# A graph network layer on one Trainium2 core: one more product by quarters in three weight matrices, a shared PSUM bank, and half of a count moved

## The chip, the cores and the metric

The kernel runs on one core of one Trainium2 chip. A core has TensorE (PE, the matrix unit), VectorE (DVE), ScalarE (ACT), GpSimd (POOL) and SyncE (SP); each works through its own instructions in order, and they wait for each other by semaphores. TensorE writes its products to PSUM, eight banks of 512 float32 columns on 128 partitions, and VectorE and ScalarE take them from there. Transfers between memory and the core's SBUF are DMAs, issued from the queues of SP, ACT and POOL. The metric is device time in microseconds (us) of one execution; lower is better. The time before is 1338.05 us, the median of three runs (1337.94 to 1341.44).

## What is computed

Rows of x are normalised and rectified to h. For each of eight edge types r, the rows of h at the sources of the edges of that type are averaged at each destination and multiplied by `weight[r]`; with `h @ root` and the bias that gives u. Then come a gate and a residual.

```python
h = jnp.maximum(_layernorm(x), 0.0)              # 1250 x 1024
out = h @ root + bias
for r in range(8):                               # 20000 edges, 8 types
    mask = (edge_type == r).astype(h.dtype)
    sums = segment_sum(h[src] * mask[:, None], dst, num_segments=1250)
    cnt = segment_sum(mask, dst, num_segments=1250)
    out = out + (sums / jnp.maximum(cnt, 1.0)[:, None]) @ weight[r]
u = out
z = jnp.concatenate([u, h], axis=1) @ w_gate + b_gate
result = x + jnp.tanh(u) * z + h * (1.0 - z)
```

## The kernel before

**Products first, gathers after.** The kernel multiplies h by each weight matrix first, stores the products y, and then gathers rows of y for the edges. Matrices 0 to 7 are `weight[0..7]`, matrix 8 is `root`, 9 and 10 are the lower and upper half of `w_gate`. The edges fall into two groups: group 0 has types 0 to 4, group 1 types 5 to 7 (`R0 = (0, 5, 8)`), so group 0 can be gathered after matrix 4, while TensorE is at matrices 5 to 7.

**One step.** The 1250 rows are ten blocks of 128 (the last one shorter). Step (m, i) multiplies blocks i and i + 5 by matrix m, for i = 0 to 4. It uses Strassen's scheme in Winograd's form: the two blocks and the halves of the inner dimension make a 2 x 2 left operand (A11, A12, A21, A22 and the sums S1 to S4, kept in `h_op`), the matrix is cut in four quarters of 512 x 512 (B11 to B22 and the sums T1 to T4), and seven products replace eight. A product is four matmuls 512 columns wide, all at L406. `product` writes them in a fixed order: A11·B11, S1·T1, S2·T2, S3·T3 and so on to A22·T4. ScalarE evicts some results to the row tiles (L457 the first, L469 S1, L489 S2, L430 S3, L529 A22), VectorE adds the others (L423, L431, L448). A row tile's half c21 holds S3's result for L431 and then gets A22's from L529.

**A second level.** In matrices 1 to 9 steps 0 and 1, and 2 and 3, make pairs. Some of their products are done for both steps of a pair at once, by quarters, by the same scheme again: seven products of two matmuls 256 columns wide (L219) in place of two products of four. `Second` does A12·B21 that way and `First` A11·B11, in all paired steps; `Third` does S4·B22, only where `thirds(s)` says so, which is s > EARLY = 3. Elsewhere S4·B22 is a plain product (`p3`, L423). The quarter products need sums of quarters from VectorE: L273 to L282 for `Third` and `First`, L207 to L215 for `Second`. `Third.first` (called from the `fill` of step 1 or 3) makes three quarter products in two banks: P1 into bank `ps_q`, copied out by ScalarE (L297); S1·T1 into a bank of the pool `ps`; S2·T2 onto P1 in `ps_q`, copied out by ScalarE (L300). `Third.last` adds three more, and `fifth_to`, `first_to` and `last_to` add the results to the rows on VectorE (L308 to L317). `First.early` and `First.late` seed a bank by ScalarE (L345, L355), and TensorE accumulates onto the seed.

**Calls.** After each product (and some fillers) `product` runs `between(j)`, j = 0 to 6; the step's `beside(j)` then issues the sums and weight loads that stand at that j and calls whatever other work runs beside the products. The order of the products, and with it the place of a call, depends on what the step has: where `first` is given, `head` is set and the fill has no "first", half of S1 comes first, then `First.late` and call 0; where the fill has a "first", S1 and call 0 come before `First.late`.

**The index.** From matrix 0 on, beside the products, `slots` gives each edge its place in a table of slots, 40 chunks of 512 edges. Each takes two phases, one a call. The first has `one_hots` (ScalarE, L1055, L1057; VectorE, L1060), loads of keys (SP) and `as_bf16` (ScalarE, L1102). The second has `look` and `count` (TensorE, bf16 matmuls into `ps_q`, L1124, L1069), `pick` and `add_counts` (VectorE, which read `ps_q`, L1132, L1077), `residue`, `place` (VectorE, L1140, L1145, and every fourth time the scatter of 16 columns of edges by GpSimd, L1163) and `to_los` (ScalarE, L1116, L1117). From matrix 1 on nothing of it is done at calls (0,0), (1,5) and (4,4). Then `order` sorts the destinations: `places` is twenty VectorE rows over 1280 columns (L1205), ten for each group, one a call; after each group GpSimd writes and reads the positions (L788, L798) and gathers the slots of the nodes (L740, `idx`). The index ends in step (4,1).

**Counts, weights, gathers.** `counts(g)` counts the edges of each node by type from `idx` (VectorE, L777, L778), `as_reciprocals` inverts the counts, `weights(g)` makes a weight for every slot. Counts of both groups run in matrix 4; then `counts_over` loads a register on every engine and skips a conditional (`tc.If`, L1533) that is for nodes with more edges than slots; then the weights run in matrices 4 and 5. From call (5,0,3) on GpSimd gathers rows of y (`add_slot`, L1339), into five buffers `got`, and VectorE adds them to u with their weights (L1344).

**Buffers.** PSUM has four banks `ps` and two `ps_b` in rotation, and `ps_n` and `ps_q`. In matrices 1 to 3 `ps_q` belongs to the index and `ps_n` is not used.

Of the kernel before, what the change touches and what calls it, by code (L numbers as in the profile page):

```python
# [19 lines left out]
def tile_rgcn_highway(  # L20
# [238 lines left out]
    class Third:  # L259
# [31 lines left out]
        def first(self, p):  # L291
            self.b = psum.tile([P, CG, P], F32, name="ps_q", bufs=1).rearrange(
                "p c k -> p (c k)")[:, :H]
            self.c = bank()[:, :H]
            self.p = p
            Second.add(self, self.b, self.a11, self.b11, True)
            nc.scalar.copy(self.p[:, :H], self.b)  # L297
            Second.add(self, self.c, self.s1, self.t1, True)
            Second.add(self, self.b, self.s2, self.t2)
            nc.scalar.copy(self.p[:, H:], self.b)  # L300

        def last(self, c):
            Second.add(self, self.b, self.s1, self.t1)
            Second.add(self, self.c0[:, H:], self.s2, self.b22)
            Second.add(self, c[:, :H], self.a22, self.t2)
# [5 lines left out]
        def fifth_to(self, to):  # L311
            nc.vector.tensor_add(to[:, H:], to[:, H:], self.c)

        def last_to(self, to, to1, c):
# [236 lines left out]
    def thirds(s):  # L551

        return s > EARLY

# [3 lines left out]

    waiting, waiting_third, waiting_first = {}, {}, {}
    at_call = [0, 0]  # L560

# [8 lines left out]
    def step(s, i, between=lambda j: None, second=None):  # L570
# [23 lines left out]
        def beside(j):  # L594
            at_call[:] = i, j
            new = fac[s + 1]
# [39 lines left out]
        def sums(j):  # L636


            e = waiting[0][0]
            for k in {2: (0, 1), 5: (2, 3)}.get(j, ()) if s > EARLY else (j,) if j < 4 else ():  # L640
                e.right(k)
            if j == (5 if s > EARLY else 4):
                e.next_left()
# [13 lines left out]
        if two:  # L657
# [98 lines left out]
    def slot_weights(g, at, w, t, drc):  # L756

        n = at.shape[2]
        for r in range(R0[g], R0[g + 1]):
# [50 lines left out]
    with ExitStack() as early:  # L810
# [161 lines left out]
        at_i = ix1.tile([P, NCH], I32, name="at_i")  # L972
        q_bank = psum.tile([P, CG, P], F32, name="ps_q", bufs=1).rearrange("p c k -> p (c k)")

# [60 lines left out]
        def slots(ix):  # L1035
# [6 lines left out]
            ng = -(-NCH // CG)  # L1042
            counted = q_bank[:, H:H + CG * NHI].rearrange("p (c b) -> p c b", b=NHI)
            looked = q_bank[:, H + CG * NHI:H + 3 * CG * NHI].rearrange(
                "p (c a b) -> p c a b", a=2, b=NHI)
# [136 lines left out]
        def order():  # L1182

            with tc.tile_pool(name="sort", bufs=1) as sp:
# [11 lines left out]
                nc.vector.memset(one, 1.0)  # L1196
                for _ in range(7):
                    yield
                pos = sp.tile([P, NHI], F32, name="pos")

                def places(g):
                    for d in range(ND):
# [4 lines left out]
                            op0=OP.is_gt, op1=OP.mult, accum_out=pos[:, c:c + 1])  # L1207
                        yield
                    nc.vector.tensor_copy(pos_i[:, g, :], pos[:, g * ND:(g + 1) * ND])
# [10 lines left out]
        def norms():  # L1220
# [59 lines left out]
            first_part.close()  # L1280

        def index():
            for _ in zip_longest(norms(), columns()):
# [23 lines left out]
    with ExitStack() as edges_part:  # L1307
# [18 lines left out]
        def counts(g):  # L1326
            t = got()
# [4 lines left out]
        def as_reciprocals():  # L1332
            nc.vector.tensor_scalar_max(rcp, rcp, 1.0)
            nc.vector.reciprocal(rcp, rcp)

# [111 lines left out]

        def beside(e, total, s, i, last):


            between = spread(e, total, 7 * ((last - s) * NP + NP - i))
            while s <= last:
                step(s, i, between)
                s, i = next(steps, (NM, 0))
            return s, i

        s, i = next(steps)
        while s <= EARLY:
            step(s, i)
            s, i = next(steps)  # L1460

        def beside_group():
# [3 lines left out]
            for _ in range(5):  # L1466
                yield
            for g in range(G):
                yield from counts(g)

        def weights_of_groups():

            as_reciprocals()
            yield
            for g in range(G):
                yield from weights(g)
                yield
            yield from passes_needed()

# [48 lines left out]

        def counts_over():

            over = nc.values_load(n_over[0:1, 0:1], min_val=0, max_val=E // MORE,
                                  skip_runtime_bounds_check_because="no more passes than edges")
            with tc.If(over > 0):  # L1533
                p = Passes()
                with tc.For_i(0, over, 1):
                    p.to_table()
                    for g in range(G):
                        slot_rows(g, more_rows, p.at)
                        for _ in slot_counts(g, p.at, p.t, p.cum, p.more):
                            pass  # L1540
                    nc.vector.tensor_add(rcp, rcp, p.more)
                    p.next()
# [6 lines left out]
        while s < R0[1]:  # L1549
            step(s, i, on)  # L1550
            s, i = next(steps)
            if (s, i) == (R0[1] - 1, NP - 1):
                for _ in ready:
                    pass
                counts_over()
                ready = weights_of_groups()

# [251 lines left out]
```

## Time and profile before

| | |
|---|---|
| median of three runs | 1338.05 us |
| the profiled execution's own time | 1337.41 us |
| its span | 1335.6 us |
| granted TensorE clock | 0.998 of full |

Windows of the profiled execution, from step (m, 0) to the next matrix (us; each engine's busy time in it):

| matrix | window | PE | DVE | ACT | POOL |
|---|---|---|---|---|---|
| 1 | 143.0 to 265.0 | 122.0 | 74.5 | 70.4 | 66.5 |
| 2 | 265.0 to 387.0 | 122.0 | 77.0 | 70.6 | 68.7 |
| 3 | 387.0 to 505.5 | 118.5 | 69.3 | 24.1 | 44.3 |
| 4 | 505.5 to 621.4 | 115.9 | 67.1 | 20.8 | 39.5 |
| 5 | 621.4 to 737.2 | 115.8 | 98.0 | 20.9 | 52.4 |

The profile has the execution of one core. "Busy" is the time in which an engine has an instruction running; L406 is line 406 of the kernel. In a timeline each line has the start, the busy time, engine, line, operation, output and inputs, shapes and how many; what stands in brackets is the idle time before it and what ended it. A float32 matmul has two records, so a product of four matmuls shows as x8. An instruction's busy time overlaps the next one's start by about 0.1 us.

### The profile page before, as it was taken

The page shows a single profiled execution, that of the slowest core. Times are in us where ns is not written, and L with a number is a line of the kernel's source. Part 1 is how long each engine was busy: PE and PEld are TensorE (multiplying, and loading weights), DVE is VectorE, ACT ScalarE, POOL GpSimd, SP SyncE. Part 2 cuts the span into 40 slices and gives each one's busy share as a digit, 9 for nine tenths or more (in the row PEclk, how much of TensorE's full clock was granted, in tenths as well). Part 3 has the DMA queues.
Part 4 walks back from the last instruction along what each step waited for, and adds up shares of the span by engine and source line. Part 5 has one row for each costly group of instructions (what it writes and reads, how often), then busy time and mean ns, then how long its engine had stood idle before and what let it go on. Part 6 is the DMA issues. An engine that isn't in the chain of part 4 may idle for free.

```text
span 1335.6 us, 13410 instructions
## 1 busy us (share of the span) xinstructions
PE 1323.3 (99%) x4168; PEld 722.1 (54%) x4168; DVE 956.9 (72%) x1823; ACT 372.7 (28%) x794; POOL 568.5 (43%) x509
## 2 busy tenths in 40 slices
PE   9999999999999999999999999999999999999997
PEld 5444555455455545655655565565556556544443
DVE  7753755674675467448987978897778889867875
ACT  3335556465641212111121121112121112221210
POOL 0000364554657036501454546346365555615631
PEclk9999999999999999999999999999999999999999
DMA  8745476866754241143738778878788957969961
GB/s 318 270 182 175 104 124 141 191 126 109 172 160 95 88 114 53 53 148 111 254 127 319 244 253 333 290 238 268 277 273 301 347 192 243 308 251 296 340 168 59
DMA packets 104319, 270.94 MB, mean 203 GB/s; under 512 B 20100, under 2 KB 22354, under 8 KB 104112
## 3 DMA queue, kind: packets, MB, share of 16 engines
q1 hardware_dynamic: 44048, 119.85, 29.3%
q0 software_dynamic: 44064, 118.20, 27.7%
q10 hardware_dynamic: 16128, 31.98, 7.7%
q8 instruction: 33, 0.54, 0.2%
q14 instruction: 46, 0.38, 0.1%
HBM read 212.63 MB, written 75.49 MB: 216 GB/s over the span
## 4 chain that ended last, share of the span: by engine, by line
PE 85%; issue 4%; DVE 2%; DMA 2%; POOL 1%; ACT 0%; POOLq 0%; DVEq 0%; ACTq 0%
PE ps_b L406 41%; PE ps L406 17%; PE ps L219 14%; PE ps_b L219 4%; PE ps_n L406 4%; PE ps_q L219 2%; PE ps_n L219 2%; PE ps_q L406 2%; DMA w<-in_L_gnn_b_gate_dram 1%; DMA h_op<-z_dram,node 1%; POOL out_dram L746 1%; DVE row L1733 0%; DVE row L1734 0%; PE ps_q L1069 0%; PE ps_q L1124 0%
## 5 line engine op out<-in xcount | busy, mean ns | idle before, releaser
L406 PE MATMUL ps_b<-w,h_op 128*128 128x512 f32 x1464 | 659.6, 595 | 1.0 <-ACT row L489 0.8
L406 PEld LDWEIGHTS ps_b<-w,h_op 128*128 128x128 f32 x1464 | 273.6, 190 | 308.4 <-issue 297.4
L1339 POOL DMA_INDIRECT got<-y,idx x193 | 245.8, 1274 | 290.3 <-DVE u L1344 184.1
L1344 DVE SCALAR_TENSOR_TENSOR u<-got,w_of,u 128x1024 f32<-128x1024 f32 (+1 forms) x193 | 246.9, 1282 | 31.8 <-DMA got<-y,idx 29.3
L406 PE MATMUL ps<-w,h_op 128*128 128x512 f32 (+1 forms) x592 | 264.8, 589 | 0.1
L1163 POOL DMA_INDIRECT table<-row_col,at_i x157 | 165.2, 1052 | 185.5 <-DVE at_i L1159 133.0
L406 PEld LDWEIGHTS ps<-w,h_op 128*128 128x128 f32 x592 | 111.0, 190 | 119.2 <-issue 115.0
L431 DVE TENSOR_TENSOR row<-row 128x512 f32<-128x512 f32 x44 | 30.3, 690 | 79.0 <-ACT row L430 79.0
L430 ACT COPY row<-ps_b 128x512 f32<-128x512 f32 x53 | 31.1, 586 | 194.1 <-PE ps_b L406 194.1
L406 PE MATMUL ps_n<-w,h_op 128*128 128x512 f32 x176 | 80.1, 592 | 0.0
L489 ACT COPY row<-ps_b 128x512 f32<-128x512 f32 x54 | 31.7, 586 | 163.6 <-PE ps_b L406 163.4
L219 PE MATMUL ps<-w,h_op 128*128 128x256 f32 x288 | 74.5, 381 | 0.0
L219 PE MATMUL ps<-w,w 128*128 128x256 f32 x288 | 71.1, 380 | 0.0
L529 ACT COPY row<-ps_b 128x512 f32<-128x512 f32 x40 | 23.4, 585 | 162.6 <-PE ps_b L406 142.3
L219 PEld LDWEIGHTS ps<-w,h_op 128*128 128x128 f32 x288 | 54.0, 190 | 27.1 <-issue 21.6
L219 PE MATMUL ps<-inner,inner 128*128 128x256 f32 x264 | 67.8, 379 | 0.0
L219 PEld LDWEIGHTS ps<-w,w 128*128 128x128 f32 x288 | 54.6, 190 | 21.8 <-issue 15.8
L219 PEld LDWEIGHTS ps<-inner,inner 128*128 128x128 f32 x264 | 50.2, 190 | 14.5 <-issue 8.4
L1145 DVE SCALAR_TENSOR_TENSOR junk<-k_bc,key_col,before 128x128 f32<-128x128 int32 x157 | 55.0, 350 | 4.2
L406 PEld LDWEIGHTS ps_n<-w,h_op 128*128 128x128 f32 x176 | 33.4, 190 | 39.5 <-issue 39.0
L457 ACT COPY row<-ps_b 128x512 f32<-128x512 f32 x54 | 31.7, 587 | 75.9 <-PE ps_b L406 71.3
L1055 ACT ACTIVATE is_lo<-io,less_lo 128x128 bf16<-128x128 f32 x157 | 50.1, 391 | 0.7 <-DMA xh_dram<-xt 0.7
(238 smaller groups left out, 1469.5 us busy)
## 6 DMA issues: line engine op xcount, KB each, us to landing
y<-row SPq DMA_DIRECT2D x72, 512.0 KB
w<-in_L_gnn_weight_dram ACTq DMA_DIRECT2D x21, 1024.0 KB
w<-in_L_gnn_weight_dram SPq DMA_DIRECT2D x10, 1024.0 KB
k_bc<-keys_dram SPq DMA_DIRECT2D x39, 256.0 KB
l_bc<-los_dram SPq DMA_DIRECT2D x39, 256.0 KB
w<-in_L_gnn_w_gate_dram ACTq DMA_DIRECT2D x6, 1024.0 KB
h_dram<-h_op SPq DMA_DIRECT2D x9, 512.0 KB
u<-in_L_gnn_bias_dram SPq DMA_DIRECT2D x9, 512.0 KB
```

What stands on the lines that cost most here:

```text
L219: nc.tensor.matmul(p, a[:, k, :], b[:, k, :], start=(fresh and k == 0), stop=(k == 1), skip_group_check=True)
L406: nc.tensor.matmul(b[:, at], aop[:, i, k, :], w.of[i][:, k, at], start=(fresh and k == 0), stop=(k == KQ - 1), skip_group_check=True)
L430: nc.scalar.copy(d, b)
L431: nc.vector.tensor_add(c22, c if lone else c22, d)
L457: nc.scalar.copy(c11, b)
L489: nc.scalar.copy(c12, b)
L529: nc.scalar.copy(c21, b)
L1055: nc.scalar.activation(is_lo[:, i, :], io, AF.Abs, bias=less_lo[:, c0 + i:c0 + i + 1])
L1145: nc.vector.scalar_tensor_tensor(junk, o["k_bc"][:, i, :], key_col[:, c:c + 1], before, op0=OP.is_equal, op1=OP.mult, accum_out=rank[:, c: ...
L1163: ins = nc.gpsimd.indirect_dma_start(out=table[:, :], out_offset=bass.IndirectOffsetOnAxis(ap=at_i[:n, c:c + 1], axis=0), in_=row_col[:n, ...
L1339: nc.gpsimd.indirect_dma_start(out=t[:n], out_offset=None, in_=y[g][:, :], in_offset=bass.IndirectOffsetOnAxis(ap=at[:n, d, k:k + 1], axis=0),
L1344: nc.vector.scalar_tensor_tensor(u[:n], t[:n], w, u[:n], op0=OP.mult, op1=OP.add)
```

## The change

`Third` now serves matrices 1 to 3 too: `thirds(s)` is s > 0. As the index holds `ps_q` there, both share its bank: `Third` has columns 0 to 255, the index those above, as long as `q_bank` is not empty (the program empties it when the index has ended, after step (4, 2), so step (4, 1) shares it too, and later matrices have it to themselves as before). Where the bank is shared (`apart`), a quarter product starts afresh instead of adding to P1, and VectorE makes the missing sums. `Third.first` is cut in two: P1 is written ahead of the other quarter products of that filler, `rest` after them. This order holds in all matrices.

```diff
         def first(self, p):
-            self.b = psum.tile([P, CG, P], F32, name="ps_q", bufs=1).rearrange(
-                "p c k -> p (c k)")[:, :H]
-            self.c = bank()[:, :H]
+            self.apart = bool(q_bank)
+            self.b = (q_bank[0] if self.apart else psum.tile([P, CG, P], F32, name="ps_q", bufs=1)
+                      .rearrange("p c k -> p (c k)"))[:, :H]
             self.p = p
             Second.add(self, self.b, self.a11, self.b11, True)
             nc.scalar.copy(self.p[:, :H], self.b)
+
+        def rest(self):
+            self.c = bank()[:, :H]
             Second.add(self, self.c, self.s1, self.t1, True)
-            Second.add(self, self.b, self.s2, self.t2)
-            nc.scalar.copy(self.p[:, H:], self.b)
+            Second.add(self, self.b, self.s2, self.t2, self.apart)
+            if self.apart:
+                nc.vector.tensor_add(self.p[:, H:], self.p[:, :H], self.b)
+            else:
+                nc.scalar.copy(self.p[:, H:], self.b)
 
         def last(self, c):
-            Second.add(self, self.b, self.s1, self.t1)
+            Second.add(self, self.b, self.s1, self.t1, self.apart)
...
         def fifth_to(self, to):
             nc.vector.tensor_add(to[:, H:], to[:, H:], self.c)
+            if self.apart:
+                nc.vector.tensor_add(to.rearrange("p (a n) -> p a n", a=2),
+                                     to.rearrange("p (a n) -> p a n", a=2),
+                                     self.p[:, None, H:].to_broadcast([P, 2, H]))
...
     def thirds(s):
 
-        return s > EARLY
+        return s > 0
...
-                fill = dict(first=lambda: (e.first(), q and q.first(t[1][:, :Q]), 0)[-1],
+                fill = dict(first=lambda: (q and q.first(t[1][:, :Q]), e.first(), q and q.rest(),
+                                           0)[-1],
...
                 fill = dict(first=lambda: (q.first(t[1][:, :Q]), e.fourth(), e.to_second(t[0]),
-                                           e.fourth_to_second(t[0]), 0)[-1],
+                                           e.fourth_to_second(t[0]), q.rest(), 0)[-1],
```

With `thirds` the steps of matrices 1 to 3 also take what the later matrices had: the order of products and fillers, the calls at which `Second` makes its sums (2 and 5), and the load of the next B11 at call (3, 1) instead of (3, 0).

The index no longer leaves out whole calls. Instead `look` waits at the calls in SHARED and `one_hots` at those in SEEDS. `places` takes two rows a call for group 0, and `order` two calls less before them.

```diff
+                    if f in (look, one_hots):
+                        while at_matrix[0] and at_call in (SHARED if f is look else SEEDS):
+                            yield
...
+        AHEAD = [[0, 6], [1, 0], [2, 6], [3, 0]]
+        SEEDS = AHEAD + [[0, 0], [1, 5], [NP - 1, 4], [NP - 1, 6]]
+        SHARED = AHEAD + [[0, 0], [1, 3], [1, 4], [3, 4], [3, 5]]
...
-                if s > 0 and (i, j) in ((0, 0), (1, 5), (NP - 1, 4)):
-                    return
...
-                for _ in range(7):
+                for _ in range(5):
                     yield
...
-                        yield
+                        if g or d % 2:
+                            yield
```

Counts and weights go by group. Group 0's counts stay in matrix 4 and its weights go to matrix 5; group 1's counts and weights go to matrix 5, beside the first gathers, which start two calls later (`LATE + 2`). `counts_over` is there once for each group: at the start of step (5, 0), with the load of the register, and at that of (5, 3). `counts` uses a buffer of the pool of u instead of one of `got`, and `weights` yields every second time.

```diff
-        first_group = with_ready(edges(0, range(ND), u_back(0), LATE))
+        first_group = with_ready(edges(0, range(ND), u_back(0), LATE + 2))
         next(first_group)
-        s, i = beside(first_group, sum(K[0]) + LATE + 1, s, i, R0[2] - 1)
+
+        def last_counts():
+            nonlocal ready
+            for _ in ready:
+                pass
+            counts_over(1)
+            ready = weights_of_last()
+
+        s, i = beside(first_group, sum(K[0]) + LATE + 3, s, i, R0[2] - 1, last_counts)
```

More of the change, by code (lines that the diff above doesn't have):

```diff
@@ L551, in thirds @@
     def thirds(s):
-        return s > EARLY
+        return s > 0
     def firsts(s):
         return s > 0
-    waiting, waiting_third, waiting_first = {}, {}, {}
-    at_call = [0, 0]
+    waiting, waiting_third, waiting_first, q_bank = {}, {}, {}, []
+    at_call, at_matrix = [0, 0], [0]
     def next_first(s, i):
@@ L594, in beside @@
         def beside(j):
-            at_call[:] = i, j
+            at_call[:], at_matrix[0] = (i, j), s
             new = fac[s + 1]
@@ L639, in sums @@
             e = waiting[0][0]
-            for k in {2: (0, 1), 5: (2, 3)}.get(j, ()) if s > EARLY else (j,) if j < 4 else ():
+            for k in {2: (0, 1), 5: (2, 3)}.get(j, ()):
                 e.right(k)
-            if j == (5 if s > EARLY else 4):
+            if j == 5:
                 e.next_left()
@@ L768, in slot_weights @@
                 nc.vector.tensor_add(w, w, t)
-                yield
+                if (r - R0[g]) % 2:
+                    yield
         nc.vector.scalar_tensor_tensor(w, at, float(FAR), w, op0=OP.is_lt, op1=OP.mult)
@@ L972, in tile_rgcn_highway @@
         at_i = ix1.tile([P, NCH], I32, name="at_i")
-        q_bank = psum.tile([P, CG, P], F32, name="ps_q", bufs=1).rearrange("p c k -> p (c k)")
+        q_bank.append(psum.tile([P, CG, P], F32, name="ps_q", bufs=1)
+                      .rearrange("p c k -> p (c k)"))
         def columns():
@@ L1042, in slots @@
             ng = -(-NCH // CG)
-            counted = q_bank[:, H:H + CG * NHI].rearrange("p (c b) -> p c b", b=NHI)
-            looked = q_bank[:, H + CG * NHI:H + 3 * CG * NHI].rearrange(
+            counted = q_bank[0][:, H:H + CG * NHI].rearrange("p (c b) -> p c b", b=NHI)
+            looked = q_bank[0][:, H + CG * NHI:H + 3 * CG * NHI].rearrange(
                 "p (c a b) -> p c a b", a=2, b=NHI)
@@ L1207, in places @@
                             op0=OP.is_gt, op1=OP.mult, accum_out=pos[:, c:c + 1])
-                        yield
+                        if g or d % 2:
+                            yield
                     nc.vector.tensor_copy(pos_i[:, g, :], pos[:, g * ND:(g + 1) * ND])
@@ L1326, in counts @@
         def counts(g):
-            t = got()
+            t = new_u(0)
             yield from slot_counts(
@@ L1330, in counts, with as_reciprocals @@
                 t[:, ND * SLOTS:ND * (SLOTS + R + 1)].rearrange("p (d r) -> p d r", r=R + 1), rcp)
-        def as_reciprocals():
-            nc.vector.tensor_scalar_max(rcp, rcp, 1.0)
-            nc.vector.reciprocal(rcp, rcp)
+        def as_reciprocals(g):
+            of = rcp[:, :, R0[g]:R0[g + 1]]
+            nc.vector.tensor_scalar_max(of, of, 1.0)
+            nc.vector.reciprocal(of, of)
         def add_slot(u, g, d, k, at, w):
@@ L1446, in passes_over, with beside @@
             nc.vector.tensor_single_scalar(n_over, top_i, 2, op=OP.arith_shift_right)
-        def beside(e, total, s, i, last):
+        def beside(e, total, s, i, last, then=None):
             between = spread(e, total, 7 * ((last - s) * NP + NP - i))
@@ L1454, in beside @@
                 s, i = next(steps, (NM, 0))
+                if (s, i) == (R0[1], 3):
+                    then()
             return s, i
@@ L1460, in tile_rgcn_highway @@
             s, i = next(steps)
+        q_bank.clear()
         def beside_group():
@@ L1467, in beside_group, with weights_of_first, weights_of_last @@
                 yield
[L1468 to L1473, printed above, removed]
+            yield from counts(0)
+        def weights_of_first():
+            as_reciprocals(0)
             yield
-            for g in range(G):
-                yield from weights(g)
+            yield from weights(0)
+            for _ in range(7):
                 yield
+            yield from counts(1)
+        def weights_of_last():
+            as_reciprocals(1)
+            yield
+            yield from weights(1)
+            yield
             yield from passes_needed()
@@ L1527, in next, with counts_over @@
                 nc.vector.tensor_single_scalar(self.done, self.done, float(-MORE), op=OP.add)
[L1529 to L1533, printed above, removed]
+        over = []
+        def counts_over(g):
+            with tc.If(over[0] > 0):
                 p = Passes()
-                with tc.For_i(0, over, 1):
+                with tc.For_i(0, over[0], 1):
                     p.to_table()
[L1537 to L1541, printed above, removed]
+                    slot_rows(g, more_rows, p.at)
+                    for _ in slot_counts(g, p.at, p.t, p.cum, p.more):
+                        pass
+                    at = slice(R0[g], R0[g + 1])
+                    nc.vector.tensor_add(rcp[:, :, at], rcp[:, :, at], p.more[:, :, at])
                     p.next()
@@ L1551, in tile_rgcn_highway @@
             s, i = next(steps)
-            if (s, i) == (R0[1] - 1, NP - 1):
+            if (s, i) == (R0[1], 0):
                 for _ in ready:
                     pass
-                counts_over()
-                ready = weights_of_groups()
+                over.append(nc.values_load(
+                    n_over[0:1, 0:1], min_val=0, max_val=E // MORE,
+                    skip_runtime_bounds_check_because="no more passes than edges"))
+                counts_over(0)
+                ready = weights_of_first()
         def with_ready(e):
@@ L1562, in with_ready @@
                 yield
-        first_group = with_ready(edges(0, range(ND), u_back(0), LATE))
+        first_group = with_ready(edges(0, range(ND), u_back(0), LATE + 2))
         next(first_group)
-        s, i = beside(first_group, sum(K[0]) + LATE + 1, s, i, R0[2] - 1)
+        def last_counts():
+            nonlocal ready
+            for _ in ready:
+                pass
+            counts_over(1)
+            ready = weights_of_last()
+        s, i = beside(first_group, sum(K[0]) + LATE + 3, s, i, R0[2] - 1, last_counts)
         passes = nc.values_load(n_pass[0:1, 0:1], min_val=0, max_val=E // MORE,
```

## The prediction

> Matrices are numbered from 0; "call (m, i, j)" is call j of step i of matrix m, and index phases are placed by the order in which the changed program's instructions stand. Times with two decimals that are not durations are positions in the profiled execution.
>
> **What bounds the kernel now.** First the head of the page: how long TensorE is busy.
>
> ```profile
> span 1335.6 us, 13410 instructions
> ...
> PE 1323.3 (99%) x4168; PEld 722.1 (54%) x4168; DVE 956.9 (72%) x1823; ACT 372.7 (28%) x794; POOL 568.5 (43%) x509
> ```
>
> Then the list of what TensorE waited for (us in total, times, longest): six waits, 4.5 us in all.
>
> ```profile
> PE ps L722 <- POOL eps L724: 1.4, 1, 1.4
> ...
> PE ps_b L219 <- ACT ps_b L345: 0.6, 1, 0.6
> ```
>
> So the end is set by the matmul stream alone. An edit is worth the TensorE time it removes, less the waits it puts into that stream; other engines' work costs nothing until TensorE waits for it. Third, TensorE's timeline, for the prices: four 512-wide matmuls (8 records) from 541.05 to 544.48 are 3.43 us, two 256-wide ones (4 records) 0.86 us. The first line is where step (4,1) writes its second quarter product.
>
> ```profile
> 527.27 1.03 PE L219 MATMUL ps_q<-inner,inner 128*128 128x256 f32 x4
> ...
> 541.05 3.60 PE L406 MATMUL ps_b<-w,h_op 128*128 128x512 f32 x8
> 544.48 1.03 PE L219 MATMUL ps<-w,h_op 128*128 128x256 f32 x4
> 545.34 1.03 PE L219 MATMUL ps<-inner,inner 128*128 128x256 f32 x4
> ```
>
> Fourth, ScalarE's timeline in matrix 1: an eviction delays what follows by 0.48 us, `to_los` (L1116, L1117) by 1.30 us (0.76 + 0.54), `one_hots` with its cast by 1.99 us (165.60 to 167.59).
>
> ```profile
> 149.61 0.59 ACT L469 COPY row<-ps 128x512 f32<-128x512 f32 x1 [2.06 <-PE ps L406]
> 150.09 0.72 ACT L1116 ACTIVATE to_lo<-l_bc,less_pid 128x512 bf16<-128x512 int32 x1
> 150.85 0.63 ACT L1117 ACTIVATE to_lo<-to_lo 128x512 bf16<-128x512 bf16 x1
> ...
> 165.11 0.59 ACT L529 COPY row<-ps_b 128x512 f32<-128x512 f32 x1 [3.22 <-PE ps_b L406]
> 165.60 1.27 ACT L1055 ACTIVATE is_lo<-io,less_lo 128x128 bf16<-128x128 f32 x4
> 166.90 0.63 ACT L1057 ACTIVATE is_lo<-is_lo 128x512 bf16<-128x512 bf16 x1
> 167.44 0.24 ACT L1102 CAST s_b<-seen 128x80 bf16<-128x80 f32 x1
> 167.59 0.58 ACT L457 COPY row<-ps_b 128x512 f32<-128x512 f32 x1
> ```
>
> Fifth, VectorE from the end of matrix 3 to the middle of step (4,0). After the 2.78 us of idleness at 505.69 it works without a gap until 525.4, and each placing row L1205 holds it for 1.47 us.
>
> ```profile
> 505.69 0.69 DVE L423 TENSOR_TENSOR row<-row,ps 128x512 f32<-128x512 f32 x1 [2.78 <-PE ps L406]
> ...
> 516.45 0.41 DVE L250 TENSOR_TENSOR row<-row,ps 128x256 f32<-128x256 f32 x1
> ...
> 521.25 0.69 DVE L431 TENSOR_TENSOR row<-row 128x512 f32<-128x512 f32 x1
> ```
>
> **Removed from TensorE.** A pair of steps had two S4·B22 products of four 512-wide matmuls, 2 x 3.43 = 6.87 us. By quarters it has seven products of two 256-wide ones, 7 x 0.86 = 6.03. Matrices 1 to 3 have two pairs each: 6 x 0.84 = **5.0 us** less. The index's own matmuls are as many as before (0.30 us for a look with a count: 275.93 to 276.15, and 0.08 on the next matmul).
>
> **Added to VectorE and ScalarE.** Per pair VectorE gets eight sums of factors (4 x 0.69 + 4 x 0.42), the additions L308, L309, L312 and three of 0.69 (L315 to L317), and two new ones for the shared bank (0.42, 0.69), and loses two additions of 0.69: about 7.7 us, 46 us in six pairs. It was busy 74.5, 77.0 and 69.3 us in matrices 1 to 3 (122, 122, 118.5 us long), so TensorE's stream covers it on average; what counts is single places. Five are exposed, each worked out from the end T of the TensorE product before it; an eviction starts T + 0.20 (product to 523.82, L529 at 524.02).
>
> A. Call (m,2,5) in matrices 1 and 2 now has `one_hots`; next comes `seventh`, whose ScalarE copy (L236) must leave the bank before `fourth` writes it. ScalarE: 0.20 + 0.49 + 1.99 + 0.37 = T + 3.05. TensorE has only `seventh` and the quarters' first product ahead: T + 1.72. Wait 1.3, twice (in matrix 3 the one-hots are done): **2.6**. Before, a 3.43 us product stood between.
>
> B. Call (m,2,0), matrices 1 to 3: with `first` filled, `product` does S1 and its call before `first.late()`. `to_los` is then ahead of the seeding copy L355 (0.57): 0.20 + 0.48 + 1.30 + 0.57 = T + 2.55. TensorE: index 0.30 and two products, T + 2.02. Wait 0.55, three times: **1.65**.
>
> C. Call (m,1,5), left out before, has a look now, so `to_los` runs ahead of `early`'s copy L345 (0.36): T + 2.34 against T + 2.02. Wait 0.35, three times: **1.05**. The one wait of before on that copy (134.32, 0.55 us) is this case at (0,4), with more index work ahead.
>
> D. (1,1): the quarters' first product shares its bank with the index and waits for `add_counts` of call (1,0,5). VectorE from the pick of call (1,0,1): 2.93 + 1.20 + 0.15 + 0.34 + 0.34 + 0.79 + 1.87 + 2.23 + 0.61 + 0.24 + 1.87 + 0.45 = 13.0 (phase with table, factor sums, additions, `left`, quarter sums, phase, L431, one-hots, sums, pick and count), begun 0.5 after the S1 product. TensorE takes 3 x 0.30 + 3 x 3.43 + 2 x 0.86 = 12.9. Wait **0.6**; no trace shows it, so 0 to 1.2.
>
> E. Step (4,0). The first group's placings move from steps (3,2) and (3,3) to calls (3,4,5) to (4,0,2), and go two to a call. One more at (3,4,5) fits into the 2.78 us. Between 505.69 and L250 VectorE did three; now it does eight, at (3,4,6) and (4,0,0) to (4,0,2): 5 x 1.47 = 7.35 us more, with no idleness to take it. L250 goes to 523.8, the quarter sums end at 527.2 (needed at 527.27: just in time), then one placing, and L431 runs at 528.7 to 529.3. L431 reads the half row that ScalarE's next eviction overwrites, so L529 starts at 529.4 instead of 524.02; behind it stand L457 and the quarters' copy L297: 529.4 + 0.48 + 0.48 + 0.37 = 530.75. TensorE's second product into that bank, ready at 527.27, waits **3.5 us**. This is the largest term.
>
> The waits are 2.6 + 1.65 + 1.05 + 0.6 + 3.5 = 9.4, less 5.0 = **+4.4 us**.
>
> The Trainium skill, PSUM — Partial Sum Buffer, "PSUM bank collisions raise a hardware error", says to guard PSUM by bank, not by address, which speaks against this sharing. By it D stands; by the rows, where index and quarters never shared a bank in these matrices, it could be nothing, and the sum +3.8. The skill's TensorE: Matmul & The Clock Gate, Part 1, has the clock halve after about one idle window of 3.4 us. The page's PEclk is 9 throughout with no wait over 1.4 us, so no row shows it; an estimate by that page is up to 1.7 us more on E.
>
> **At nothing.** Half the counting goes from matrix 4 to 5: three pairs L777, L778 of 0.75 us and small rows, 2.5 us, where VectorE is busy 98.0 of 115.8 us. A second conditional: the one of before cost VectorE 0.93 us (idle to 595.13, released by the branch at L1533) and TensorE no row in its list of waits; cover gone, up to 1 us each. GpSimd must see its gathers landed there; it stands up to five buffers ahead and VectorE's longest wait for one was 3.7 us: 0 to 1. The later index: positions and slots of a group took GpSimd 46 us (479.5 to 525.5); from 527 they land by 573, the counts that read them stand at about 593. The load of B11 one call later has 3.4 us less of some 27.
>
> **The rivals.** R1, no wait: 1338.05 - 5.0 = 1333.0, faster. For it: matrices 5 to 8 run the quarters without one wait. Against: they have no index on ScalarE (20.9 us busy a matrix, against 70 in 1 and 2). It decides if the waits sum below 1 us. R2, not slower: only one kind of wait. If VectorE finds 3.5 us of room before L431 at (4,0), E is gone: -5.0 + 5.9, 1338.9. For it only the idleness before 505.69, which is already used up. If ScalarE's order is kinder and only E stays, -1.5: 1336.6. R3: all of it, and what stands at nothing on top, the conditionals and the gathers with up to 3 us: 1343.4 to 1345.4. For it: two conditionals in place of one. Against: TensorE showed no wait at the one. That the change doesn't cut the products is excluded: 48 wide matmuls fewer and 84 narrow more stand in the program.
>
> **How the numbers follow.** Against the profiled execution's 1337.41 the sum gives 1341.8; the median of the runs shown is 0.64 higher, so 1342.4. 0.3%, what a measurement of this kernel can tell from no change, is 4.0 us, just inside the sum. Chances: the forecast 0.64, of which 0.52 over that bound and 0.12 under; R1 0.08; R2 0.20 (0.01 faster); R3 0.08. Faster 0.09, same 0.31, slower 0.60. Waits of 7 to 12 us give the forecast's own range, 1340 to 1345; with R2 and R3, 1336.5 to 1345.5.
>
> **What would show it.** TensorE busy 5 us less in all; matrices 1 and 2 about as long as before, 122 us (2.6 to 3 us of waits against 1.7 saved); new entries in TensorE's waits: one of about 3.5 us on ScalarE's quarter copy near 530, two of about 1.3 on the copy of `seventh`, three each on L345's and L355's copies. An L529-like eviction released by VectorE's L431 there shows E right. No such entry, and a span below 1332, would make the forecast wrong.

## The result, and the profile after

The changed kernel takes **1346.04 us** (median of five runs, 1345.39 to 1347.16); beside it the kernel before took 1338.05 (1337.45 to 1341.44). The ratio is 1.0053, 95% interval 1.0039 to 1.0068: slower by 8.0 us. The forecast was 1342.4, so the sign was right and the size 3.6 us short; the median lies 0.5 us above the upper end of the range. The span grew by 8.6 us, from 1335.6 to 1344.2.

Lines moved down a little: L406 of before is L416 now, L345 and L355 are L355 and L365, L431 is L441, L529 is L539, L1116 and L1117 are L1129 and L1130. First the head of the page of the changed kernel, then its list of what TensorE waited for (us in total, times, longest).

```profile
span 1344.2 us, 13675 instructions
...
PE 1322.1 (98%) x4240; PEld 737.2 (55%) x4240; DVE 998.0 (74%) x1911; ACT 373.2 (28%) x799; POOL 582.5 (43%) x509
```

```profile
PE ps_q L219 <- DVE junk L1221: 3.3, 1, 3.3
PE ps L219 <- ACT w L236: 2.5, 2, 1.3
PE ps L381 <- DVE h_op L874: 1.7, 1, 1.7
PE ps L733 <- POOL eps L735: 1.4, 1, 1.4
PE ps_b L219 <- ACT ps_b L365: 1.2, 3, 0.4
PE ps_b L219 <- ACT ps_b L355: 1.1, 4, 0.6
PE ps_b L416 <- ACT row L499: 0.8, 1, 0.8
PE ps L381 <- DVE h_op L386: 0.7, 1, 0.7
PE ps_q L219 <- DVE seen L1090: 0.5, 1, 0.5
PE ps L219 <- DVE inner L274: 0.4, 1, 0.4
PE ps_b L416 <- ACT h_op L388: 0.2, 1, 0.2
```

Every wait the forecast named is there, with its number of times: one on the quarters' bank near 530 (E; the list puts it down to the placing row L1221, which ended at the same moment as the bank's copy L297, at 533.7), two on L236 (A), three on L365 (B), three new ones on L355 (C; the fourth is the one of before), one on the index count (D). One was not named, on L274. The list has grown from 4.5 to 13.8 us.

But TensorE is busy only 1.2 us less, where 5.0 were to go. The timeline of TensorE at wait E tells why:

```profile
529.27 1.10 PE L219 MATMUL ps<-inner,inner 128*128 128x256 f32 x4 [0.36 <-DVE inner L274]
533.70 2.07 PE L219 MATMUL ps_q<-inner,inner 128*128 128x256 f32 x4 [3.33 <-DVE junk L1221]
535.57 4.37 PE L416 MATMUL ps<-w,h_op 128*128 128x512 f32 x8
539.77 1.89 PE L219 MATMUL ps<-w,w 128*128 128x256 f32 x8
```

The product behind the wait takes 2.07 us where the same form took 1.03 before, and the wide one after it 4.37 instead of 3.60. The windows there have the reason (window, its length, then busy us and instructions of TensorE, weight loads, VectorE, ScalarE and GpSimd, then TensorE's granted clock, the share of the transfers and GB/s):

```profile
530.40:533.65 3.25, 0.00 (x0) 0.00 (x0) 3.25 (x6) 1.35 (x4) 2.44 (x2) 1.00 0.01 0
533.69:537.10 3.41, 3.40 (x6) 2.18 (x7) 3.37 (x7) 0.51 (x2) 2.80 (x3) 0.50 0.44 159
537.11:540.00 2.89, 2.89 (x9) 1.34 (x8) 2.85 (x3) 0.03 (x1) 2.28 (x3) 1.00 0.01 0
```

After 3.3 idle us the clock is 0.50 for 3.41 us. From the restart at 533.70 to the product at 539.77 are 6.07 us; behind a shorter wait in the same place they are 4.40 (579.30 to 583.70, shown below): **1.67 us** for the half clock, counted as busy time. Busy time hides two more things. An idle time of the list is about 0.16 us shorter than the delay from one start to the next (the product before it is drained meanwhile), and the first product after a wait takes 0.10 longer (1.13 against 1.03). So the account is made from start to start, over TensorE's whole stream:

| term | forecast | measured |
|---|---|---|
| fewer and narrower matmuls | -5.0 | -4.9 |
| A, L236 in (m,2,5), two | 2.6 | 1.45 + 1.36 = 2.8 |
| B, L365 in (m,2,0), three | 1.65 | 3 x 0.58 = 1.7 |
| C, L355 in (m,1,5), three | 1.05 | 3 x 0.36 = 1.1 |
| D, index count in (1,1) | 0.6 | 0.7 |
| E, the quarters' bank at (4,1) | 3.5 | 3.5 |
| L274 at (4,1) | 0 ("just in time") | 0.5 |
| half clock behind E | 0 (named as up to 1.7) | 1.7 |
| eleven restarts | 0 | 11 x 0.10 = 1.1 |
| the rest (first products and end 0.8 later; index matmuls and rounding 0.5 less) | 0 | 0.3 |
| sum | 4.4 | 8.5 of 8.6 |

The 0.8 at the ends lies in work that the change doesn't touch; a single profile can't tell it from scatter.

ScalarE's and VectorE's timelines show E as it was drawn. L539 used to start at the end of its product; now it starts when VectorE has read the half row (L441, behind nine placing rows L1221 since the start of step (4,0), where it was four), with L467 and the quarters' copy L297 behind it. The first two lines are the first two of the nine: two rows in a row stand 1.59 us apart, not 1.47.

```profile
510.72 1.55 DVE L1221 SCALAR_TENSOR_TENSOR junk<-v_bc,val,one 128x1280 bf16<-128x1280 f32 x1
...
512.31 1.55 DVE L1221 SCALAR_TENSOR_TENSOR junk<-v_bc,val,one 128x1280 bf16<-128x1280 f32 x1
...
530.05 1.55 DVE L1221 SCALAR_TENSOR_TENSOR junk<-v_bc,val,one 128x1280 bf16<-128x1280 f32 x1
...
531.52 0.69 DVE L441 TENSOR_TENSOR row<-row 128x512 f32<-128x512 f32 x1
```

```profile
532.30 0.58 ACT L539 COPY row<-ps_b 128x512 f32<-128x512 f32 x1 [9.85 <-DVE row L441]
532.78 0.59 ACT L467 COPY row<-ps_b 128x512 f32<-128x512 f32 x1
533.26 0.39 ACT L297 COPY row<-ps_q 128x256 f32<-128x256 f32 x1
```

And A, in matrix 1: the one-hots (L1068, L1070) and the cast stand ahead of the copy that `fourth` needs.

```profile
214.64 0.58 ACT L539 COPY row<-ps_b 128x512 f32<-128x512 f32 x1 [3.33 <-PE ps_b L416]
215.12 1.28 ACT L1068 ACTIVATE is_lo<-io,less_lo 128x128 bf16<-128x128 f32 x4
216.42 0.63 ACT L1070 ACTIVATE is_lo<-is_lo 128x512 bf16<-128x512 bf16 x1
216.96 0.33 ACT L1115 CAST s_b<-seen 128x20 bf16<-128x20 f32 x2
217.20 0.36 ACT L236 COPY w<-ps 128x256 f32<-128x256 f32 x1
```

### The profile page after: what moved, and what is told of

Read it like the earlier page. It is cut to its first block, busy times and chain, and to the rows that moved or that the text cites. A ratio compares the mean times of both kernels' runs of the same rounds, so it can differ in the third digit from the quotient of the medians.

```text
span 1344.2 us, 13675 instructions
## 1 busy us (share of the span) xinstructions
PE 1322.1 (98%) x4240; PEld 737.2 (55%) x4240; DVE 998.0 (74%) x1911; ACT 373.2 (28%) x799; POOL 582.5 (43%) x509
## 4 chain that ended last, share of the span: by engine, by line
PE 84%; issue 4%; DVE 3%; ACT 2%; POOL 2%; POOLq 0%; DVEq 0%; ACTq 0%
PE ps_b L416 40%; PE ps L219 14%; PE ps L416 12%; PE ps_n L416 5%; PE ps_b L219 3%; PE ps_q L219 3%; PE ps_n L219 2%; PE ps_q L416 2%; DVE junk L1221 1%; POOL out_dram L757 1%; POOL got L751 0%; PE ps L381 0%; ACT to_lo L1129 0%; ACT is_lo L1068 0%; PE ps_q L1082 0%
## 5 line engine op out<-in xcount | busy, mean ns | idle before, releaser
L416 PE MATMUL ps_b<-w,h_op 128*128 128x512 f32 x1464 | 659.4, 595 | 1.0 <-ACT row L499 0.8
L416 PEld LDWEIGHTS ps_b<-w,h_op 128*128 128x128 f32 x1464 | 274.6, 190 | 304.1 <-issue 294.1
L1359 POOL DMA_INDIRECT got<-y,idx x193 | 255.9, 1326 | 238.1 <-DVE u L1364 173.1
L1176 POOL DMA_INDIRECT table<-row_col,at_i x157 | 173.3, 1104 | 242.6 <-DVE at_i L1172 138.7
L416 PE MATMUL ps<-w,h_op 128*128 128x512 f32 (+1 forms) x448 | 199.8, 588 | 0.1
L416 PEld LDWEIGHTS ps<-w,h_op 128*128 128x128 f32 x448 | 84.9, 191 | 92.4 <-issue 89.8
L416 PE MATMUL ps_n<-w,h_op 128*128 128x512 f32 x224 | 102.3, 593 | 0.0
L499 ACT COPY row<-ps_b 128x512 f32<-128x512 f32 x54 | 31.6, 585 | 166.6 <-PE ps_b L416 166.4
L219 PE MATMUL ps<-inner,inner 128*128 128x256 f32 x288 | 74.3, 381 | 0.4 <-DVE inner L274 0.4
L416 PEld LDWEIGHTS ps_n<-w,h_op 128*128 128x128 f32 x224 | 42.5, 190 | 48.7 <-issue 48.2
L539 ACT COPY row<-ps_b 128x512 f32<-128x512 f32 x40 | 23.4, 584 | 161.3 <-PE ps_b L416 120.0
L219 PEld LDWEIGHTS ps<-w,h_op 128*128 128x128 f32 x288 | 54.2, 190 | 23.4 <-issue 13.7
L219 PEld LDWEIGHTS ps<-inner,inner 128*128 128x128 f32 x288 | 54.5, 190 | 14.2 <-issue 6.9
L441 DVE TENSOR_TENSOR row<-row 128x512 f32<-128x512 f32 x44 | 30.3, 688 | 42.0 <-ACT row L440 42.0
L1158 DVE SCALAR_TENSOR_TENSOR junk<-k_bc,key_col,before 128x128 f32<-128x128 int32 x157 | 55.1, 351 | 4.2
L467 ACT COPY row<-ps_b 128x512 f32<-128x512 f32 x54 | 31.7, 587 | 77.0 <-PE ps_b L416 73.3
L1068 ACT ACTIVATE is_lo<-io,less_lo 128x128 bf16<-128x128 f32 x157 | 50.0, 391 | 0.8 <-DMA xh_dram<-xt 0.8
```

Of the source, the lines that this page charges most:

```text
L219: nc.tensor.matmul(p, a[:, k, :], b[:, k, :], start=(fresh and k == 0), stop=(k == 1), skip_group_check=True)
L416: nc.tensor.matmul(b[:, at], aop[:, i, k, :], w.of[i][:, k, at], start=(fresh and k == 0), stop=(k == KQ - 1), skip_group_check=True)
L441: nc.vector.tensor_add(c22, c if lone else c22, d)
L467: nc.scalar.copy(c11, b)
L499: nc.scalar.copy(c12, b)
L539: nc.scalar.copy(c21, b)
```

## The experiments

All kernels start from the changed one. They ran in three sets. The set of f0 to f3 ran where the kernel before takes 1337.8 us, as in the first comparison. The changed kernel itself was not run again there, so "less than the changed kernel" compares two sets, whose kernels before differ by 0.3 us. The sets of e1 to e4 and of g1 to g4 ran on two other chips, where it takes 1389.6 and 1389.0. Their traces show TensorE waits of up to 9.4 us in matrices 1 to 4 that the others don't have: ScalarE and VectorE stand still, for up to 13.6 and 15.0 us at a time, and the trace puts the end of that down to another core or an unknown queue (more on that at the end of the next section). There the times tell little, and single places are read instead.

**The placings one to a call (E).** The pause after each row of the first group is restored, and the order's last pause is shortened so that the passes stay where they were.

```diff
-                        if g or d % 2:
-                            yield
+                        yield
...
-                for _ in range(3):
-                    yield
+                yield
```

> The first group's placings one to a call, as before (and one pause for three at the end of the order, so that the passes stand where they stood). Theory: the 3.33 us wait on the quarter copy near 530 is VectorE being eight placings late; now four stand before L250 instead of eight, 4 x 1.47 = 5.9 us fewer, so that wait (3.49 from start to start), the 0.52 on L274 and the slow matmuls behind it (1.7) all go: 1346.0 - 5.8 = 1340.2, granted clock 1.00 throughout. Rival one, the wait has another cause (the copy's own queue): no change, 1346. Rival two, the gathers of positions and slots, five calls (17 us) later, are late for the counts of matrix 4 and TensorE waits there: 1342 to 1346 with a new wait near 600 to 625.

> The kernel with the placings one to a call, once more, to be read beside the others. Theory: 5.8 us less than the changed kernel, ratio to the kernel before 1.001, no wait near (4,1) and no half clock there. Rival: the gathers, 17 us later, are late for the counts of matrix 4 and TensorE waits near the end of matrix 4.

e1_single: 1397.73, ratio 1.0047 (1.0025 to 1.0069); no wait at (4,1) and full clock there, but a wait of 9.4 us near the end of matrix 4, on a copy (L499) that came late after such a standstill. f0_single: **1339.78**, ratio 1.0013 (1.0004 to 1.0022), 6.3 us less than the changed kernel, 5.8 forecast; no wait in matrix 4 at all. Its TensorE timeline at the place of E:

```profile
528.64 1.03 PE L219 MATMUL ps<-inner,inner 128*128 128x256 f32 x4
529.50 1.03 PE L219 MATMUL ps_q<-inner,inner 128*128 128x256 f32 x4
530.37 3.60 PE L416 MATMUL ps<-w,h_op 128*128 128x512 f32 x8
```

Nothing is waited for, and the clock is 1.00. Five placing rows stand ahead of L441 there, not nine. So E, with what it draws behind it, comes from the four that two to a call put there, and the gathers 17 us later cost nothing (rival two falls).

**Is it the clock?** Two kernels keep wait E and change its idle time. e2_dose leaves one placing fewer ahead of L441. e3_busy puts seven matmuls that nobody reads into the idle time. Both were run again as g2_dose and g1_busy.

```diff
-                        if g or d % 2:
+                        if g or d % 2 or d == 8:
```

```diff
             self.c = bank()[:, :H]
+            if at_matrix[0] == R0[1] - 1 and at_call[0] < 2:
+                for _ in range(7):
+                    nc.tensor.matmul(self.c, self.a11[:, 0, :], self.b11[:, 0, :],
+                                     start=True, stop=True)
```

> One placing fewer ahead of the row addition L441 (8 instead of 9 since the start of step (4,0)), nothing else. The wait near 530 shrinks by 1.6 us, to about 1.7, and the 0.52 on L274 goes. Theory (the half clock is set off by the length of the idle time): at 1.7 us of idleness the clock stays at 1.00, so 1.7 more are saved: 1.6 + 0.5 + 1.7 = 3.8, 1342.2. Rival (the matmuls behind the wait are slow for a reason that is there at any wait in this place, the transfers at full rate or the refill): they stay slow, 1.6 + 0.5 = 2.1, 1343.9.

> Seven 128x256 matmuls whose result nobody reads are put into the wait near 530 (3.0 us of work in 3.85 us of two waits); what TensorE waits for is not touched, so the product behind the wait starts when it did. Theory: TensorE is then never idle for more than 1 us there, the clock is not halved, and the products behind the wait run at full speed: 1.7 us less, 1344.3, no part of the run at clock 0.50 before the end. Rival (transfers, or the start after a wait as such, make them slow): the matmuls behind stay slow and the time is 1346.0, or up to 0.4 more.

> The changed kernel with one placing fewer ahead of L441, once more, for its time. Theory: the idle time near 530 is 2.4 us (VectorE 1.4 us earlier, ScalarE's copies 0.5 each behind L441), the clock stays at 1.00 unless that stretch fills most of one of the clock's steps of 3.41 us; with it 0.9 + 0.6 + 1.7 = 3.2 us less than the changed kernel, 1342.8, ratio 1.0038. Rival (any wait here is followed by slow matmuls): 1.5 less, 1344.5, ratio 1.0050.

> The changed kernel with the seven matmuls that nobody reads in the wait near 530, once more, for its time beside the others. Theory: what TensorE waits for stays where it was, the product behind the wait starts when it did, but no part of the run is at clock 0.50 there: 1.7 us less than the changed kernel, 1344.3, ratio to the kernel before 1.0049. Rival: the matmuls behind the wait stay slow and the time is that of the changed kernel, 1346.0, ratio 1.0062.

Ratios: 1.0062 (1.0037 to 1.0086), 1.0097 (1.0060 to 1.0135), 1.0063 (1.0043 to 1.0083) and 1.0071 (1.0041 to 1.0102); these intervals are too wide for 1.7 us, so no time decides here. The traces do. TensorE's timeline of e2_dose, then of e3_busy (where L416 has become L420):

```profile
579.30 1.13 PE L219 MATMUL ps_q<-inner,inner 128*128 128x256 f32 x4 [2.38 <-ACT row L297]
580.27 3.60 PE L416 MATMUL ps<-w,h_op 128*128 128x512 f32 x8
583.70 1.89 PE L219 MATMUL ps<-w,w 128*128 128x256 f32 x8
```

```profile
580.37 3.19 PE L303 MATMUL ps<-w,h_op 128*128 128x256 f32 x14
583.39 1.03 PE L219 MATMUL ps<-inner,inner 128*128 128x256 f32 x4
585.32 1.13 PE L219 MATMUL ps_q<-inner,inner 128*128 128x256 f32 x4 [0.90 <-ACT row L297]
586.29 3.60 PE L420 MATMUL ps<-w,h_op 128*128 128x512 f32 x8
```

In both, and in both repeats, the products behind the wait take 1.13 and 3.60 us at clock 1.00. e4_los, from the same set and with E untouched, has the idle 3.33 us and the half clock again. So the slow products come from TensorE's idle time: a refill that any wait has would have stayed, and so would the transfers, which ran at 155 GB/s behind e2_dose's wait and at 159 in the changed kernel. How much idle time it takes isn't told by these four; the last section shows that the place of the 2.38 us helped too. What failed is a size: the idle time of e2_dose was to be 1.7 us and was 2.38. L441 came 1.6 us sooner as expected, but without the wait on L274 TensorE came 0.5 sooner too, and waited that much longer.

**`to_los` out of two calls (B, C).** It is done at the start of the next call.

```diff
+            held = []
...
                     if f is None:
                         yield
+                        while held:
+                            to_los(held.pop())
+                    elif f is to_los and at_matrix[0] and at_call in ([1, 5], [2, 0]):
+                        held.append(of)
```

> The two activations of to_los are taken out of calls (m,1,5) and (m,2,0) of matrices 1 to 3 and done at the start of the next call; everything else stays in its call. Theory: the waits on the copies L355 (three of 0.36 from start to start) and L365 (three of 0.58) are these 1.30 us ahead of the copy: all six go, with 0.1 each for the refill: 1.1 + 1.7 + 0.6 = 3.4, 1342.6. Rival: the 1.30 us one call later hold the next copies on ScalarE (L479 in call (m,1,6), L225 and L227 in (m,2,1)), and TensorE waits there instead: less than 1.5 gained, 1344.5 to 1346.

> Placings one to a call and to_los moved, one_hots left where the change put it. Theory: 5.8 + 3.4 = 9.2 us less than the changed kernel, 3.0 more than with all three moves, ratio to the kernel before 0.9995; in TensorE's waits only the two on L236 and the one on L1090 are new. Rival (the index work moved collides): new waits on L479, L225 or L499 in matrices 1 to 3 and a ratio over 1.002.

e4_los: 1399.57, ratio 1.0071 (1.0040 to 1.0102). In its trace the three waits on L355 in (m,1,5) are gone; one of 2.2 us stays on L365 in matrix 2, behind a wait of 2.7 us on L280 that the traces of those two chips alone have. f3_single_los, with the placings one to a call as well: **1336.50**, ratio 0.9989 (0.9980 to 0.9999), 3.3 us less than f0_single, 3.4 forecast, and all six waits gone; no new one on L479, L225 or L499.

**`one_hots` out of call (m,2,5) (A).**

```diff
+            later = []
...
+                    if f is one_hots and at_matrix[0] and at_call == [2, 5] and of < ng:
+                        later.append(of)
+                        continue
                     if f in (look, one_hots):
                         while at_matrix[0] and at_call in (SHARED if f is look else SEEDS):
                             yield
+                        while later:
+                            one_hots(later.pop())
```

> Only one_hots of call (m,2,5) is moved, to call (m,3,1), in matrices 1 and 2. Theory: the two waits on the copy L236 (1.45 and 1.36 from start to start, 0.1 each of refill) are its 1.99 us ahead of that copy: both go, nothing else changes, 3.0 us less than the changed kernel. Rival: the wait goes to the copy L297 of the quarters two products later, or to L499 in call (m,3,1), and less than 1 us is won.

f1_hots: **1343.32**, ratio 1.0042 (1.0027 to 1.0058), 2.7 us less than the changed kernel, 3.0 forecast. Both waits on L236 are gone and none took their place; E and its half clock (530.35 to 533.76) are still there.

**All three moves.**

> Three moves together: placings one to a call, to_los out of calls (m,1,5) and (m,2,0), and one_hots out of call (m,2,5) into (m,3,1). Theory (the changed kernel is 5.0 us of matmuls saved and given back by waits of ScalarE and VectorE, each of which has its own place): of the 11 new waits only the one on the index count (L1090, 0.71) is left, against before -4.9 + 0.8 = -4.1 us, a ratio of 0.997, and the granted clock stays at 1.00 up to the end wherever it does so in the kernel before. Rival one (something else of the change costs time: the second conditional, the later index, the gathers): no better than the kernel before, ratio 1.000 or more. Rival two (the moved index work makes new waits of the same size): ratio 1.001 to 1.004.

f2_all: **1333.59** (1333.47 to 1333.94), ratio 0.9968 (0.9956 to 0.9980): 4.2 us less than the kernel before, 4.1 forecast, 2.9 less than f3_single_los. Its head and its list of TensorE's waits:

```profile
PE 1318.5 (99%) x4240; PEld 736.9 (55%) x4240; DVE 997.8 (75%) x1911; ACT 374.1 (28%) x799; POOL 584.4 (44%) x509
```

```profile
PE ps L733 <- POOL eps L735: 1.4, 1, 1.4
PE ps_b L416 <- ACT row L499: 0.8, 1, 0.8
PE ps L381 <- DVE h_op L874: 0.7, 1, 0.7
PE ps L381 <- DVE h_op L386: 0.7, 1, 0.7
PE ps_q L219 <- DVE seen L1090: 0.6, 1, 0.6
PE ps_b L219 <- ACT ps_b L355: 0.6, 1, 0.6
PE ps_b L416 <- ACT h_op L388: 0.2, 1, 0.2
```

This is the list of before and one line more, D. TensorE is busy 4.8 us less than before, as the matmuls alone say. So on this chip nothing else of the change costs anything that can be seen, the second conditional and the later index among it.

**The last wait (D).** All three moves, and the table of call (1,0,1) done in call (1,0,5) behind the count.

```diff
-                    to_table(j // AT * AT * CG, c0 + m)
+                    tables.append((j // AT * AT * CG, c0 + m))
+                while tables and (at_matrix[0], at_call) != (1, [0, 1]) and \
+                        (at_matrix[0], at_call) != (1, [0, 3]):
+                    to_table(*tables.pop())
...
+            tables = []
```

> All three moves and one more: the four operations of the table after call (1,0,1), 0.58 us of VectorE from the first to the next instruction, done in call (1,0,5) behind the index count. Theory: the one new wait left, on L1090 in matrix 1 (0.71 from start to start), is VectorE's time ahead of that count, so 0.58 of it goes: 1333.0, ratio 0.9964. Rival: the count waits for its matmuls and not for VectorE's queue, or L304 and the sums behind it come late: nothing won, 1333.6 or more.

The wait went from 0.55 to 0.46 us only: a miss. VectorE's timeline shows where the 0.58 went: into idle time ahead of L250. The lines are g3_tables', then f2_all's.

```profile
153.39 0.23 DVE L1073 TENSOR_TENSOR is_at<-hi_col,io 128x80 bf16<-128x80 f32 x1
154.29 0.42 DVE L250 TENSOR_TENSOR row<-row,ps 128x256 f32<-128x256 f32 x1 [0.66 <-ACT row L499]
```

```profile
154.21 0.23 DVE L1073 TENSOR_TENSOR is_at<-hi_col,io 128x80 bf16<-128x80 f32 x1
154.41 0.42 DVE L250 TENSOR_TENSOR row<-row,ps 128x256 f32<-128x256 f32 x1
```

In f2_all L250 stands behind L1073 without a pause, and yet it did not move: in both traces it starts 1.12 us after the start of a product of TensorE into `ps` (153.17 in g3_tables, 153.29 in f2_all). ScalarE's row, which the view names, was there 0.3 us earlier in g3_tables (L499, 153.37 + 0.58). So what delays the count is the VectorE work behind L250, and taking away work ahead of it buys nothing; the 0.09 lie behind L250, where one row (L1158) took 0.42 us in f2_all and 0.35 here, and can be scatter. On that chip the kernel took 1394.74, ratio 1.0041 (1.0015 to 1.0067).

**The counts back in matrix 4.** All three moves, with both groups' counts, one conditional and the weights as before the change.

```diff
-            yield from counts(0)
+            for g in range(G):
+                yield from counts(g)
...
-            for _ in range(7):
-                yield
-            yield from counts(1)
...
-            counts_over(1)
```

> All three moves, but the counts and weights of the second group are put back into matrix 4, with one conditional instead of two. Theory: the second conditional and the moved counts cost TensorE nothing in the changed kernel, so taking them back wins nothing; the second group's positions and slots are fetched until 612.4 and the counts would now read them from 610 on, so VectorE waits up to 5 us near the end of matrix 4 and TensorE 0 to 3 of them: 1333.6 to 1336.6. Rival: the second conditional costs, up to 1 us for each of three engines: 1332.6 or less.

1397.15, ratio 1.0047 (1.0025 to 1.0068). TensorE has no wait from 643 to 1148 us, through the counts, the conditional and matrix 5. It has one of 8.1 us before that, on L499 after such a standstill; that delay also gave the gathers 8 us more, so that the wait that was expected for them is neither shown nor excluded. What it shows is that counts and conditional cost TensorE nothing in this place either.

## Why the prediction was right, and where short

- **What bounds the kernel, and the saving**: right. 5.0 forecast, 4.9 in the changed kernel from start to start, 4.8 in the busy time of f2_all.
- **A, B, C, D, E**: right in place and number of times, A, B, C and E in their cause too. The sizes were 2.6, 1.65, 1.05, 0.6 and 3.5 and came out as 2.8, 1.7, 1.1, 0.7 and 3.5. A, B with C, and E were taken away one at a time, and the time followed within 0.5 us. D was not taken away; that the count waits for VectorE's work is read from the trace. It stands, so the quarters do wait for the index in their shared bank: of the two values the one by the Trainium skill's PSUM — Partial Sum Buffer, "PSUM bank collisions raise a hardware error", was the right one. What would come without that wait no run shows.
- **What failed**: three costs left out of the sum. The half clock behind E was named with an estimate of up to 1.7 us and then kept out, because no wait over 1.4 us stood in the profile of before; 1.67 came. That a profile doesn't show a mechanism was no evidence against it, when the change itself made the first idle time long enough. The restarts (0.10 each, eleven of them) could be read before: 0.10 is what the first product takes longer at the one wait of that kind in matrix 0. And "the quarter sums end at 527.2 (needed at 527.27: just in time)" was a margin of 0.07 us taken as safe; L274 came 0.5 late. The price of 1.47 for a placing row was taken from rows that stood alone. Two in a row are 1.59 apart, which happens five times ahead of L250: 0.6 us that the sum lacked. They moved L250 and L441 by 0.6, and because TensorE, held up by L274, was 0.6 later as well, E still came out at 3.5. That size was right by luck.
- **The range** ended at 1345.5 because its upper end was rival R3, built from conditionals and gathers. R3's number was nearly right and its cause wrong: conditionals and gathers cost nothing, and the clock and the restarts made up the difference.
- **R1 and R2** fall: no wait was absent. "Matrices 1 and 2 about as long as before, 122 us" held: 123.0 (143.75 to 266.70) and 121.9. "TensorE busy 5 us less" didn't show, since half clock, restarts and drained products count as busy.

Open: why two chips show the standstills. They fall at about the same places in all eight runs (on ScalarE near 212, 259, 338, 379, 465 and, in all but one, 514 us). There g3_tables, which is f2_all and one move more, is slower than the kernel before (1.0041), so that the three moves beat it is shown for one chip only. The label "another core or an unknown queue" can be read further: in all eight traces the semaphore that ends a standstill of more than 2 us is one that TensorE counts up. In e4_los ScalarE's copies L225 and L227 start at 209.37 and 212.20, while the records of the products that they copy end at 200.03 and 200.89. No run tells why TensorE's word comes 9 to 11 us late there.

## What to carry to other kernels

When TensorE sets the end and an edit makes the matmuls narrower, the cover of each copy shrinks with them: work out for each copy what now stands ahead of it on ScalarE, and what the last reader of its target is. Price a wait from start to start, add 0.1 us for each restart, and look whether an idle time comes near 0.6 of the clock's step of 3.41 us; there half the clock is the next cost. Here the saving was real, and on the one chip where that was run, spreading the placings and moving two more pieces of index work to later calls kept it.

## What the runs showed of the hardware

The clock goes by steps of 3.41 us. Ten traces have half-clock stretches ahead of the run's end (the changed kernel's, f1_hots' and the eight of the two other chips). Each stretch is one, two or three steps long, and within a run all begin at multiples of 3.413 us from each other. It is not the length of a single idle time alone that decides. In e2_dose an idle time of 2.07 us halved the clock and one of 2.38 didn't. Two windows on such steps of that run, with the clock as the third number from the end, then two more:

```profile
176.04:179.45 3.41, 1.34 (x5) 0.28 (x3) 1.24 (x6) 2.90 (x9) 0.00 (x0) 1.00 0.00 0
179.45:182.86 3.41, 3.41 (x8) 2.76 (x9) 3.17 (x13) 3.35 (x9) 0.00 (x0) 0.50 0.13 44
...
575.40:578.81 3.41, 1.53 (x8) 0.99 (x6) 3.41 (x6) 0.91 (x2) 0.16 (x1) 1.00 0.00 0
578.81:582.20 3.39, 2.90 (x9) 1.82 (x10) 3.39 (x7) 0.99 (x4) 2.78 (x3) 1.00 0.39 155
```

The first idle time lay wholly in one step, which was idle for 0.61 of its length; the second was cut in two, 0.55 and 0.14. In one step it would have been 0.70, so e2_dose kept its clock by luck of the place as well. Over the ten traces every step at full clock that was idle for 0.60 of its length or more was followed by a half-clock step, none with 0.55 or less, and between them it went both ways (0.56 and 0.58 were, 0.57 and 0.59 were not). The way back asks for more: a half-clock step that was idle for 0.21 or more was followed by another, one with 0.17 or less by full clock. The Trainium skill, TensorE: Matmul & The Clock Gate, Part 1, has a free-running window of 3413 ns, and the traces agree with it; where it speaks of one idle window, 0.6 of a window was enough here.
